# Transposed tiles written back by halves, with four buffers, a later share and smaller loads, in a convolution-attention kernel

## The chip, the cores and the metric

The kernel runs on one core of one Trainium2 chip, as one program with one launch. The metric is the device time of a whole execution in microseconds (us). The kernel before took 1756.65, 1762.4 and 1763.76 us in three runs, so 1762.4 us at the median.

## The reference, cut to what matters

There are four images (B = 4) of 32 channels and 128 x 128 pixels. Layer 0 gathers each 2 x 2 patch of pixels, so that an image has 4096 positions of 128 values, and lets every position attend to all others by the cosine between them. Layer 1 takes the same data as 4096 tokens of 128 values: linear attention over 8 heads, then a mixture of 8 experts of which each token takes 2.

```python
xs = x.reshape(B, C, h, R, w, R).transpose(0, 1, 3, 5, 2, 4).reshape(B, C * R * R, h, w)
q = xs.reshape(B, C * R * R, hw)
...
energy = jnp.einsum('bci,bcj->bij', q, q)
d = jnp.sqrt(jnp.diagonal(energy, axis1=1, axis2=2))
energy = energy / (d[:, :, None] * d[:, None, :])
attn = jax.nn.softmax(energy, axis=-1)
out = jnp.einsum('bcj,bij->bci', q, attn)
out = gamma * out + xs
...
K = jnp.einsum('bnd,hkd->bhnk', x, Wk)
Q = jnp.einsum('bnd,hkd->bhnk', x, Wq)
V = jnp.einsum('bnd,hed->bhne', x, Wv)
KtV = jnp.einsum('bhnk,bhne->bhke', K, V)
out = jnp.einsum('bhnk,bhke->bne', Q, KtV)
...
top_p, top_i = jax.lax.top_k(router_probs, K)
top_p = top_p / jnp.sum(top_p, axis=-1, keepdims=True)
expert_out = jnp.einsum('bnd,edc->bnec', x, expert_w) + expert_b
gathered = jnp.take_along_axis(expert_out, top_i[..., None], axis=2)
return jnp.einsum('bnk,bnkc->bnc', top_p, gathered)
...
t = t + _L1_attn_ref(_ln_t(t), L1_attn_Wk, L1_attn_Wq, L1_attn_Wv)
t = t + _L1_ffn_ref(_ln_t(t), L1_ffn_router_w, L1_ffn_router_b, L1_ffn_expert_w, L1_ffn_expert_b)
```

`energy` is a 4096 x 4096 matrix for each image, and symmetric. Its softmax needs no maximum, since the entries are cosines, so the kernel computes exponentials, sums them by rows and divides at the end. Tokens are normalised ahead of both parts of layer 1, and each part is added to them.

## The kernel before

**Tiling.** The 4096 positions of an image are cut into NCH = 8 chunks of CH = 512, and each chunk into NJ = 4 blocks of 128. Since the matrix of exponentials is symmetric, only the lower half of the chunk pairs is computed: for row i the columns jc = 0 to i (`attend`, L417). One step is one block of 128 x 512: a product on TensorE into `pe` (L556), the exponential on ScalarE into `pr` with its row sum (L559), and the product with the values on TensorE into `po` (L440). Each of these products is float32 and is two matmul records in the profile.

**The transposed half.** A chunk pair off the diagonal also counts for the row jc with its transpose. The transpose is made in two stages. VectorE transposes `pr` by blocks of 32 x 32 into `F` (L369, reached through L566), four instructions for a tile of four steps. The blocks are then put in their places by a way through DRAM: SP issues one DMA that writes the tile (1 MB) to the DRAM tensor `blocks` (`move`, L483), and after it has landed four DMAs that read it back to `G` (`bring`, L491), each to 32 partitions. TensorE then multiplies `G` with the values into `pg`, one block at a time (`transposed_share`, L375); ScalarE sums its rows (L380), and VectorE adds the finished share to the row's output `o` (L385). The diagonal pair goes the same way in a smaller form (`below`, `diagonal_share`).

**Order.** The order of the work on TensorE, VectorE, ScalarE and SP is written out by hand, and each of these engines works through its own in that order. `tick` counts steps; `after(n, f)` issues f that many steps later: the values after 2, the DVE transpose after 1, the write of a tile 2 after its last exponential and the read 3 after that. `clock` counts units of TensorE work, 8 for a step and 4 for a block of a share. A share is put into the list `late` and is due `LAG` = 57 units after its read is issued; one block of it is run at each step (`step_share`, L411), in the order of the list. In the last row of the last image the tiles jc = 3 and 4 do without DRAM: 16 DMAs each move the blocks from F to G directly (L476, `last`), and their shares are due 58 units later. The last two tiles of that row are computed twice instead.

**Buffers.** F and G have three buffers of 8 KB per partition each (`fpool`, `gpool`), `pr` six, `blocks` four. `F`'s are also used by the diagonal and by the end of the kernel, `G`'s also by the `tmp` tiles of the end (L1152).

**What runs beside it.** While image b is in `attend`, other work is woven in as generators. `timed` holds them with a begin and an end in per cent of the image's work and a number of pieces: `prep` of the next image (loads xx by `load_tokens`, four DMAs of 128 KB each, and makes the normalised vectors), `input_rows` (loads the tokens T of the image in four parts of four DMAs), and in image 0 `setup_weights` and `setup_sorting`, which copies the input to two DRAM tensors `xs` in eight parts of 624 KB issued from ScalarE's queue. `steady` holds layer 1 of the image before: from 84% of an image `layer1` closes its rows (`close_rows`), computes the attention, routes the tokens, sorts them by expert through DRAM with indirect DMAs issued by GpSimd (L988, L1113), and stores its output through SP (L1095). Image 3's own layer 1 is done after its attention, by `last_parts`, without sorting.

Of the kernel before, what the change touches and what calls it, by code (L numbers as in the profile page):

```python
# [12 lines left out]
F32 = mybir.dt.float32  # L13
# [9 lines left out]
def kernel(  # L23
# [39 lines left out]

    nc = tc.nc
    P = 128
    B, C, H, W = x.shape
# [15 lines left out]
    big1 = ctx.enter_context(tc.tile_pool(name="big1", bufs=1))  # L85
    opool = ctx.enter_context(tc.tile_pool(name="opool", bufs=NCH))
    ppool = ctx.enter_context(tc.tile_pool(name="ppool", bufs=6))
    fpool = ctx.enter_context(tc.tile_pool(name="fpool", bufs=3))
    gpool = ctx.enter_context(tc.tile_pool(name="gpool", bufs=3))
    work = ctx.enter_context(tc.tile_pool(name="work", bufs=2))  # L90
    stat = ctx.enter_context(tc.tile_pool(name="stat", bufs=2))
    dram = ctx.enter_context(tc.tile_pool(name="dram", bufs=2, space=bass.MemoryType.DRAM))
# [43 lines left out]
    def setup_sorting():  # L136
        def iota(dst, pattern, part=0):
            nc.gpsimd.iota(
                dst, pattern=pattern, base=0, channel_multiplier=part, allow_small_or_imprecise_dtypes=True
            )  # L140

        iota(rank_below, [[1, P]], part=-1)
        nc.vector.tensor_scalar(rank_below, rank_below, 0.0, None, ALU.is_gt)
        iota(upto, [[1, E], [-1, E]])
        nc.vector.tensor_scalar(upto, upto, 0.0, None, ALU.is_ge)
        iota(tiles_of[:, 0, :], [[P, HR]])
        iota(tile_no[:, :, 0], [[1, NT]])
# [134 lines left out]
    def prep(b, kc, st):  # L282
# [17 lines left out]

        def load_half(g, pt):
# [51 lines left out]
    tick = [0]  # L353
    queued = []
    late = []
    LAG = 57
    exps = []

    BELOW = {1: 0, 2: 1, 3: 3}
# [10 lines left out]

    def transposed_share(b, st, i, jc, G):

        pg = ps_g.tile([P, CH], F32, tag="pg", name=f"pg_{b}_{i}_{jc}")
        for ib in range(NJ):
            nc.tensor.matmul(  # L375
                pg.rearrange("p (a f) -> p a f", a=4), st["qT"][i][:, ib, :], G[:, :, ib],
                start=(ib == 0), stop=(ib == NJ - 1),
            )
            junk = work.tile([P, 4, P], BF16, tag="junk", name=f"junk_{b}_{i}_{jc}_{ib}", bufs=1)
# [37 lines left out]
    def attend(b, st):  # L417
# [11 lines left out]
        for i in range(NCH):  # L429
# [37 lines left out]
                    at += P * ib  # L467
                done()

            def move(F, i, jc):  # L470
                last = b == B - 1 and i == NCH - 1 and jc >= NCH - 5
                if last:
                    G = gpool.tile([P, 4, NJ, P], F32, tag="G", name=f"G_{b}_{i}_{jc}")
                    for a in range(4):
                        for q in range(4):
                            nc.sync.dma_start(  # L476
                                G[ts(q, S), a].rearrange("p ib f -> p (ib f)"),
                                F[ts(a, S), q].rearrange("p ib j c -> p (ib j c)"),
                            )
# [3 lines left out]
                nc.sync.dma_start(  # L483
                    blocks.rearrange("a p q f -> (a p) q f"), F.rearrange("p q ib j c -> p q (ib j c)")
                )
                after(3, partial(bring, blocks, i, jc))

            def bring(blocks, i, jc):
                G = gpool.tile([P, 4, NJ, P], F32, tag="G", name=f"G_{b}_{i}_{jc}")
                for q in range(4):  # L490
                    nc.sync.dma_start(  # L491
                        G[ts(q, S)].rearrange("p a ib f -> p a (ib f)"), blocks[:, :, q].rearrange("a p f -> p a f")
                    )
# [34 lines left out]
            for jc in order:  # L528
# [13 lines left out]
                    step_share()  # L542
                    yield
                if jc < i and not both:
                    F = fpool.tile([P, 4, NJ, NJ, S], F32, tag="F", name=f"F_{b}_{i}_{jc}")
                    Fb = F.rearrange("p q ib j c -> p ib q j c")
                elif jc == i and not ending:
                    F = fpool.tile([P, 4, 6, S], F32, tag="F", name=f"F_{b}_{i}_{i}")
                own = []
                for j in range(NJ):  # L550
# [12 lines left out]
                        st["exps"] = True  # L563
                    after(2, partial(values, pr[:, c0:], t, c0, CH))
                    if jc < i and not both:
                        after(1, partial(nc.vector.transpose, Fb[:, :, :, j, :], pr))  # L566
                        if j == NJ - 1:
                            after(2, partial(move, F, i, jc))
                    elif jc == i and not ending:
                        if j < NJ - 1:  # L570
                            after(1, partial(turn_blocks, F, pr, j))
                        if j == NJ - 2:
                            after(2, partial(move_diagonal, F, i))
                    elif jc == i and j in (1, 2):

                        after(1 if j == 2 and order[-1] == i else 2, partial(below, own, (2, 1) if j == 1 else (3,)))
# [742 lines left out]
    for b in range(B):  # L1319

        if b == 0:
            for kc, begin, end in ((1, 0, 5), (2, 6, 20), (3, 25, 45)):
                timed.append((prep(0, kc, states[0]), begin, end, 12))
            timed.append((setup_weights(), 46, 58, 9))
            timed.append((setup_sorting(), 58, 98, 9))
        if b + 1 < B:
            nxt = states[b + 1]
            timed.append((prep(b + 1, 0, nxt), 65, 82, 13))
            timed.append((prep(b + 1, 1, nxt), 83, 99, 13))
        timed.append((input_rows(b, states[b]), *((55, 75) if b in (0, B - 1) else (82, 99)), 9))  # L1330
        done = [0] * len(timed)
        start = clock[0]
        closing = None
# [67 lines left out]
```

## Time and profile before

| | |
|---|---|
| median of three runs | 1762.4 us |
| the profiled execution's own time | 1753.19 us |
| its span, first to last instruction | 1751.4 us |
| granted TensorE clock, mean | 0.983 |
| DMA: bytes moved, mean rate | 355.24 MB, 203 GB/s |
| queue of SP (q1): packets, share of the 16 DMA engines | 219792, 64.0% |
| writes of tiles to DRAM (L483) | 108 of 1024 KB |
| reads of tiles from DRAM (L491) | 432 of 256 KB |
| direct moves (L476) | 32 of 64 KB |
| loads of T and of xx on SP (L279) | 64 and 62 of 128 KB |

The profile is of one execution. A row of its groups names the line, the engine, the operation and the tile written and those read, then the count, the busy time and the mean of one, and then the idle time of the engine just ahead of these instructions with what ended it. TensorE's busy time is modelled from pipelined matmuls: how many of them lie in a stretch says more than the busy share. DMA issues of SP are listed with their tiles; a DMA that SP issues late because it waits delays all that stand behind it in SP's order. The packets of the DMA engines are recorded with queue, size and duration.

### The profile page before, as it was taken

The numbers are of one execution on the slowest core, as the hardware profiler recorded it, in microseconds if no ns is written. First come the engines' busy times: TensorE is split into PE (matmuls) and PEld (weight loads), VectorE is DVE, ScalarE is ACT, GpSimd is POOL, SyncE is SP. The second block draws the span as 40 slices with busy tenths as digits, with TensorE's granted clock in tenths as the row PEclk, the third lists the DMA queues.
The fourth block names the chain that finished last, engine by engine and source line by source line (L and its number), as shares of the span: only waits on it lengthen the run. The fifth ranks groups of instructions, "written<-read, shape, count | busy, mean of one in ns | idle before, by whom it ended". The sixth has DMA issues, their size and how long they took to land. (4 is left out here: it accounts for less than half of the span.)

```text
span 1751.4 us, 21197 instructions
## 1 busy us (share of the span) xinstructions
PE 1667.8 (95%) x5458; PEld 882.2 (50%) x5458; DVE 939.7 (54%) x2443; ACT 927.0 (53%) x2893; POOL 512.0 (29%) x553
## 2 busy tenths in 40 slices
PE   8999998999999999899999999979999999899887
PEld 5444444455554455445554455535555455444633
DVE  4433333467485335566477334546748533455687
ACT  3555444466565555446565455536556455445376
POOL 1000000011026505540015622552102660463166
PEclk9999999999999999999999999989999999999989
DMA  4675877776568799997567799998656889995001
GB/s 136 195 207 166 217 200 222 237 212 190 165 195 239 232 276 252 264 243 197 164 189 223 227 273 264 251 244 224 192 166 196 251 223 271 265 267 133 1 13 37
DMA packets 240168, 355.24 MB, mean 203 GB/s; under 512 B 26928, under 2 KB 154928, under 8 KB 226096
## 3 DMA queue, kind: packets, MB, share of 16 engines
q1 hardware_dynamic: 219792, 314.91, 64.0%
q0 software_dynamic: 12288, 25.19, 5.1%
q10 hardware_dynamic: 7968, 13.77, 2.7%
q8 instruction: 46, 0.75, 0.2%
q14 instruction: 74, 0.61, 0.1%
HBM read 183.64 MB, written 173.15 MB: 204 GB/s over the span
## 5 line engine op out<-in xcount | busy, mean ns | idle before, releaser
L559 ACT ACTIVATE pr<-pe 128x512 f32<-128x512 f32 (+1 forms) x576 | 322.3, 560 | 546.3 <-PE pe L556 427.9
L440 PE MATMUL po<-pr,qT 128*128 128x512 f32 (+3 forms) x1152 | 553.2, 562 | 3.9 <-ACT o L445 3.5
L375 PE MATMUL pg<-G,qT 128*128 128x512 f32 x880 | 456.8, 601 | 37.5 <-DMA G<-blocks 25.6
L556 PE MATMUL pe<-qn,qn 128*128 128x512 f32 x896 | 464.7, 601 | 1.9 <-ACT pr L559 1.6
L369 DVE STREAM_TRANSPOSE F<-pr 128x512 f32<-128x512 f32 x440 | 305.9, 702 | 169.6 <-ACT pr L559 152.2
L440 PEld LDWEIGHTS po<-pr,qT 128*128 128x128 f32 x1152 | 217.1, 192 | 252.6 <-issue 224.8
L380 ACT ACTIVATE junk<-G 128x512 bf16<-128x512 f32 x440 | 273.1, 621 | 33.9 <-DMA G<-blocks 27.3
L375 PEld LDWEIGHTS pg<-G,qT 128*128 128x128 f32 x880 | 167.3, 192 | 239.6 <-issue 205.8
L1113 POOL DMA_INDIRECT yb<-ys,place x192 | 185.1, 964 | 275.6 <-DMA xn<-xs 103.2
L988 POOL DMA_INDIRECT xs<-xn,place x192 | 185.6, 967 | 125.5 <-issue 51.6
L556 PEld LDWEIGHTS pe<-qn,qn 128*128 128x128 f32 x896 | 156.0, 193 | 113.9 <-issue 103.5
L385 DVE TENSOR_TENSOR o<-o,pg 128x512 f32<-128x512 f32 x110 | 75.4, 685 | 201.4 <-PE pg L375 170.1
L164 POOL TENSOR_TENSOR rn<-ss,neg_half 128x8 f32<-128x8 f32 (+1 forms) x17 | 27.8, 1634 | 401.6 <-DVE ss L325 401.6
L559 ACT ACTIVATION_READ_ACCUMULATOR pr<-pe 128x1 f32 x576 | 112.1, 195 | 0.0
L1022 ACT ACTIVATE xn<-pys 128x256 f32<-128x256 f32 (+1 forms) x120 | 44.9, 376 | 116.1 <-PE pys L1055 69.3
L1048 PEld LDWEIGHTS pys<-ew_sb,xn 128*128 128x128 f32 x468 | 67.9, 191 | 57.2 <-issue 45.3
L164 POOL TENSOR_TENSOR rsf<-dm_f,neg_half 128x8 f32<-128x8 f32 (+1 forms) x15 | 26.2, 1746 | 235.1 <-DVE sv_f L635 235.1
L556 PE MATMUL pe<-qn 128*128 128x512 f32 (+3 forms) x256 | 90.2, 435 | 0.7 <-ACT qn L344 0.7
L380 ACT ACTIVATION_READ_ACCUMULATOR junk<-G 128x1 f32 x440 | 84.4, 192 | 0.0
L1048 PE MATMUL pys<-ew_sb,xn 128*128 x468 | 71.8, 276 | 11.4 <-ACT xn L1022 5.4
L1031 DVE COPY result<-pys 128x256 f32<-128x256 f32 (+1 forms) x60 | 24.6, 410 | 101.6 <-ACT xn L1022 46.2
L164 POOL TENSOR_TENSOR rsa<-dm_a,neg_half 128x8 f32<-128x8 f32 x16 | 26.4, 1647 | 167.4 <-DVE sv_a L635 167.1
(189 smaller groups left out, 1618.5 us busy)
## 6 DMA issues: line engine op xcount, KB each, us to landing
blocks<-F SPq DMA_DIRECT2D x108, 1024.0 KB
G<-blocks SPq DMA_DIRECT2D x432, 256.0 KB
xn<-xs SPq DMA_DIRECT2D x114, 128.0 KB
below<-F SPq DMA_DIRECT2D x31, 384.0 KB
G<-below SPq DMA_DIRECT2D x124, 96.0 KB
T<-in_x_dram SPq DMA_DIRECT2D x64, 128.0 KB
out_dram<-acc SPq DMA_DIRECT2D x128, 64.0 KB
xx<-in_x_dram SPq DMA_DIRECT2D x62, 128.0 KB
```

The costliest lines, as they stand in the source:

```text
L164: pinned(nc.gpsimd.tensor_tensor(dst, src, neg_half.to_broadcast(list(src.shape)), ALU.pow))
L369: f()
L375: nc.tensor.matmul(pg.rearrange("p (a f) -> p a f", a=4), st["qT"][i][:, ib, :], G[:, :, ib], start=(ib == 0), stop=(ib == NJ - 1),)
L380: nc.scalar.activation(junk, G[:, :, ib], AF.Copy, accum_out=st["sums"][:, NJ * i + ib, jc : jc + 1])
L385: nc.vector.tensor_tensor(o, o, pg.rearrange("p (a j c) -> p a j c", a=4, c=S), ALU.add)
L440: nc.tensor.matmul(row["po"][:, lo:hi], qT[blk // NJ][:, blk % NJ, :], w, start=start, stop=(row["left"] == 0))
L556: nc.tensor.matmul(pe[:, c0:], qn[jc][:, ts(j, P)], qn[i][:, c0:], start=True, stop=True)
L559: nc.scalar.activation(pr[:, c0:], pe[:, c0:], AF.Exp, accum_out=sums[:, t, i : i + 1]).ins
L988: inst = nc.gpsimd.indirect_dma_start(xs[h], offset(place[:, i, k : k + 1]), xn[:, k, :], None)
L1022: nc.scalar.activation(bufs[4 + g % 2][:, :n], p[:, : n * P].rearrange("p (j t) -> p j t", t=P), AF.Copy)
L1048: nc.tensor.matmul(p[:, 2 * P + j * D : 2 * P + j * D + D], bufs[4 + g % 2][:, j, :], weights[:, bass.ds(begins[2 * (g % 2) + j], D)], sta ...
L1113: inst = nc.gpsimd.indirect_dma_start(yb[k // 4][:, i, k % 4, :], None, ys, offset(place[:, i, k : k + 1]))
```

## The change

A tile of F becomes two half tiles, each of two transposed steps, with four buffers of 4 KB per partition. Each half is written to DRAM by its own DMA as soon as its second transpose is done (`write_half`), to every other kilobyte of `blocks`; the read (`bring`) stays at the tick where it was, five after the last exponential, and waits for both. G keeps its size, has four buffers, and its elements stand in another order within a partition, so that L375 and L380 read runs of 64 elements where they read runs of 128. The share is due 76 units after the read (`LAG`), in the last row of the last image 57 (`LAST_LAG`). The direct moves are gone: those two tiles go through DRAM as well. T and xx are loaded in halves of 64 KB per DMA (the first load of all excepted), the copies to xs in 16 parts, and the loads of T in images 0 and 3 are spread over other stretches. `pr` has six buffers, before and after.

```diff
-    fpool = ctx.enter_context(tc.tile_pool(name="fpool", bufs=3))
-    gpool = ctx.enter_context(tc.tile_pool(name="gpool", bufs=3))
+    fpool = ctx.enter_context(tc.tile_pool(name="fpool", bufs=4))
+    gpool = ctx.enter_context(tc.tile_pool(name="gpool", bufs=4))
...
-        step = NT * P // 4
-        for g in range(8):
-            inst = nc.scalar.dma_start(xs[g // 4][ts(g % 4, step), :], rows[ts(g, step), :])
-            xs_made[g // 4].append(inst.ins)
+        step = NT * P // 8
+        for g in range(16):
+            inst = nc.scalar.dma_start(xs[g // 8][ts(g % 8, step), :], rows[ts(g, step), :])
+            xs_made[g // 8].append(inst.ins)
...
-        load_tokens(
-            xx.rearrange("p k w r -> p k (w r)"), b, 8 * kc, 8, (nc.sync, nc.scalar if first else nc.sync)
-        )
+        rows = xx.rearrange("p k w r -> p k (w r)")
+        if first:
+            load_tokens(rows, b, 0, 8, (nc.sync, nc.scalar))
+        else:
+            load_tokens(rows[:, :4], b, 8 * kc, 4)
...
         yield
         yield
+        if not first:
+            load_tokens(rows[:, 4:], b, 8 * kc + 4, 4)
...
-    LAG = 57
+    LAG = 76
+    LAST_LAG = 57
...
-                pg.rearrange("p (a f) -> p a f", a=4), st["qT"][i][:, ib, :], G[:, :, ib],
+                pg.rearrange("p (a g f) -> p a g f", a=4, g=2), st["qT"][i][:, ib, :], G[:, :, :, ib],
...
-                junk, G[:, :, ib], AF.Copy, accum_out=st["sums"][:, NJ * i + ib, jc : jc + 1]
+                junk, G[:, :, :, ib], AF.Copy, accum_out=st["sums"][:, NJ * i + ib, jc : jc + 1]
...
-            def move(F, i, jc):
-                last = b == B - 1 and i == NCH - 1 and jc >= NCH - 5
-                if last:
-                    G = gpool.tile([P, 4, NJ, P], F32, tag="G", name=f"G_{b}_{i}_{jc}")
-                    for a in range(4):
-                        for q in range(4):
-                            nc.sync.dma_start(
-                                G[ts(q, S), a].rearrange("p ib f -> p (ib f)"),
-                                F[ts(a, S), q].rearrange("p ib j c -> p (ib j c)"),
-                            )
-                    late.append((clock[0] + 58, transposed_share(b, st, i, jc, G)))
-                    return
-                blocks = dram.tile([4, S, 4, CH], F32, tag="blocks", name=f"blocks_{b}_{i}_{jc}", bufs=4)
+            def write_half(blocks, F, g):
                 nc.sync.dma_start(
-                    blocks.rearrange("a p q f -> (a p) q f"), F.rearrange("p q ib j c -> p q (ib j c)")
+                    blocks[:, :, :, g].rearrange("a p q f -> (a p) q f"), F.rearrange("p q ib j c -> p q (ib j c)")
                 )
-                after(3, partial(bring, blocks, i, jc))
 
             def bring(blocks, i, jc):
-                G = gpool.tile([P, 4, NJ, P], F32, tag="G", name=f"G_{b}_{i}_{jc}")
+                G = gpool.tile([P, 4, 2, NJ, 2 * S], F32, tag="G", name=f"G_{b}_{i}_{jc}")
...
-                late.append((clock[0] + LAG, transposed_share(b, st, i, jc, G)))
+                late.append((clock[0] + (LAST_LAG if ending else LAG), transposed_share(b, st, i, jc, G)))
...
-                    F = fpool.tile([P, 4, NJ, NJ, S], F32, tag="F", name=f"F_{b}_{i}_{jc}")
-                    Fb = F.rearrange("p q ib j c -> p ib q j c")
+                    blocks = dram.tile([4, S, 4, 2, CH // 2], F32, tag="blocks", name=f"blocks_{b}_{i}_{jc}", bufs=4)
...
-                        after(1, partial(nc.vector.transpose, Fb[:, :, :, j, :], pr))
-                        if j == NJ - 1:
-                            after(2, partial(move, F, i, jc))
+                        if j % 2 == 0:
+                            F = fpool.tile([P, 4, NJ, 2, S], F32, tag="F", name=f"F_{b}_{i}_{jc}_{j // 2}")
+                        after(1, partial(nc.vector.transpose, F.rearrange("p q ib j c -> p ib q j c")[:, :, :, j % 2, :], pr))
+                        if j % 2:
+                            after(2, partial(write_half, blocks, F, j // 2))
+                            if j == NJ - 1:
+                                after(5, partial(bring, blocks, i, jc))
...
-        for kc in range(4):
-            load_tokens(T[:, ts(kc, 8), :], b, 8 * kc, 8)
+        for k in range(0, KT, 4):
+            load_tokens(T[:, k : k + 4, :], b, k, 4)
...
-            timed.append((setup_sorting(), 58, 98, 9))
+            timed.append((setup_sorting(), 58, 98, 17))
...
-        timed.append((input_rows(b, states[b]), *((55, 75) if b in (0, B - 1) else (82, 99)), 9))
+        timed.append((input_rows(b, states[b]), *((52, 94), (82, 99), (82, 99), (52, 80))[b], 17))
```

More of the change, by code (lines that the diff above doesn't have):

```diff
@@ L375, in transposed_share @@
             nc.tensor.matmul(
-                pg.rearrange("p (a f) -> p a f", a=4), st["qT"][i][:, ib, :], G[:, :, ib],
+                pg.rearrange("p (a g f) -> p a g f", a=4, g=2), st["qT"][i][:, ib, :], G[:, :, :, ib],
                 start=(ib == 0), stop=(ib == NJ - 1),
             )
-            junk = work.tile([P, 4, P], BF16, tag="junk", name=f"junk_{b}_{i}_{jc}_{ib}", bufs=1)
+            junk = work.tile([P, 4, 2, 2 * S], BF16, tag="junk", name=f"junk_{b}_{i}_{jc}_{ib}", bufs=1)
             nc.scalar.activation(
-                junk, G[:, :, ib], AF.Copy, accum_out=st["sums"][:, NJ * i + ib, jc : jc + 1]
+                junk, G[:, :, :, ib], AF.Copy, accum_out=st["sums"][:, NJ * i + ib, jc : jc + 1]
             )
@@ L468, in below @@
                 done()
-            def move(F, i, jc):
-                last = b == B - 1 and i == NCH - 1 and jc >= NCH - 5
-                if last:
-                    G = gpool.tile([P, 4, NJ, P], F32, tag="G", name=f"G_{b}_{i}_{jc}")
-                    for a in range(4):
-                        for q in range(4):
-                            nc.sync.dma_start(
-                                G[ts(q, S), a].rearrange("p ib f -> p (ib f)"),
-                                F[ts(a, S), q].rearrange("p ib j c -> p (ib j c)"),
-                            )
-                    late.append((clock[0] + 58, transposed_share(b, st, i, jc, G)))
-                    return
-                blocks = dram.tile([4, S, 4, CH], F32, tag="blocks", name=f"blocks_{b}_{i}_{jc}", bufs=4)
+            def write_half(blocks, F, g):
                 nc.sync.dma_start(
-                    blocks.rearrange("a p q f -> (a p) q f"), F.rearrange("p q ib j c -> p q (ib j c)")
+                    blocks[:, :, :, g].rearrange("a p q f -> (a p) q f"), F.rearrange("p q ib j c -> p q (ib j c)")
                 )
-                after(3, partial(bring, blocks, i, jc))
             def bring(blocks, i, jc):
-                G = gpool.tile([P, 4, NJ, P], F32, tag="G", name=f"G_{b}_{i}_{jc}")
+                G = gpool.tile([P, 4, 2, NJ, 2 * S], F32, tag="G", name=f"G_{b}_{i}_{jc}")
                 for q in range(4):
                     nc.sync.dma_start(
-                        G[ts(q, S)].rearrange("p a ib f -> p a (ib f)"), blocks[:, :, q].rearrange("a p f -> p a f")
+                        G[ts(q, S)].rearrange("p a g ib f -> p a (g ib f)"),
+                        blocks[:, :, q].rearrange("a p g f -> p a (g f)"),
                     )
-                late.append((clock[0] + LAG, transposed_share(b, st, i, jc, G)))
+                late.append((clock[0] + (LAST_LAG if ending else LAG), transposed_share(b, st, i, jc, G)))
             def move_diagonal(F, i):
```

## The prediction

> **What bounds the kernel now.** I read the busy shares first, then the groups of TensorE's instructions with the idle time ahead of each, then busy time by 25 us windows, and last TensorE and SP in order of time around one of the worst windows.
>
> ```profile
> PE 1667.8 (95%) x5458; PEld 882.2 (50%) x5458; DVE 939.7 (54%) x2443; ACT 927.0 (53%) x2893; POOL 512.0 (29%) x553
> L440 PE MATMUL po<-pr,qT 128*128 128x512 f32 (+3 forms) x1152 | 553.2, 562 | 3.9 <-ACT o L445 3.5 <-issue 0.4
> L375 PE MATMUL pg<-G,qT 128*128 128x512 f32 x880 | 456.8, 601 | 37.5 <-DMA G<-blocks 25.6 <-issue 7.0 <-DVE rdx L699 2.4
> ```
>
> TensorE is the bound with 95%, and nearly half of the 84 us that it idles stands before one matmul, the share of a transposed tile (L375), which waits for G to come back from DRAM. Ahead of the other two matmuls of a step (L440, L556) it idles 6.5 us in all.
>
> ```profile
> 325.00:350.00 25.00, 25.00 (x69) 11.81 (x68) 10.51 (x19) 11.68 (x36) 0.00 (x0) 1.00 0.83 244
> 250.00:275.00 25.00, 17.57 (x41) 7.65 (x41) 5.46 (x8) 8.01 (x24) 0.00 (x0) 0.92 0.91 249
> 725.00:750.00 25.00, 22.45 (x51) 10.19 (x51) 10.33 (x21) 9.17 (x29) 14.62 (x16) 0.87 0.98 249
> 1150.00:1175.00 25.00, 17.27 (x41) 7.59 (x40) 13.67 (x31) 8.01 (x24) 14.10 (x14) 0.87 1.01 249
> ```
>
> First PE busy and matmul count, last the granted clock, the share of the DMA engines and GB/s. Undisturbed, 69 matmul records fit in 25 us; in the late rows of images 0, 1 and 2 it is 41 to 51, and just there the clock falls to 0.87 to 0.92 and the DMA engines are 91% to fully busy.
>
> ```profile
> 1164.54 1.02 PE L556 MATMUL pe<-qn,qn 128*128 128x512 f32 x2
> 1165.39 1.02 PE L440 MATMUL po<-pr,qT 128*128 128x512 f32 x2
> 1172.70 2.04 PE L375 MATMUL pg<-G,qT 128*128 128x512 f32 x2 [6.29 <-DMA G<-blocks]
> 1174.54 1.91 PE L556 MATMUL pe<-qn,qn 128*128 128x512 f32 x2
> 1176.25 1.91 PE L440 MATMUL po<-pr,qT 128*128 128x512 f32 x2
> ```
>
> ```profile
> 1156.27 0.34 SPq L483 DMA_DIRECT2D blocks<-F  x1
> 1156.73 3.31 SPq L1095 DMA_DIRECT2D out_dram<-acc  x4
> 1162.32 2.09 SPq L491 DMA_DIRECT2D G<-blocks  x4
> 1164.51 0.38 SPq L483 DMA_DIRECT2D blocks<-F  x1
> ```
>
> A 512-column matmul (two records) starts 0.85 to 0.86 us after the last one; after a stall of 6.29 us the next ones start 1.7 to 1.84 us apart for some 5 us. A stall is thus paid twice. SP issues in order: the tile's write at 1156.3, its read 6 us later, when the write has landed, and the next tile's write behind that read.
>
> In TensorE's order of time 14 gaps over 0.8 us stand before L375 up to 1585 us: 9.5 us in image 0 (the longest 6.0), 10.4 in image 1, 13.0 in image 2, 4.2 in image 3; sum 37.1. The clock at half speed behind them costs, from the clock records of the trace (half of 3.4 to 10.2 us each, less what lies in a gap), 4.4, 4.9, 4.7 and 1.7: sum 15.7. So 13.9, 15.3, 17.7 and 5.9: **52.8 us** is the ceiling for a change of this round trip.
>
> [...] each read at L491 fills 32 partitions, and the four of a tile take 5.5 to 6.2 us of packet time when alone, 170 to 190 GB/s. [...] here the read's first packet comes about 1.5 us after the write's last. [...] before has no packet of 1 KiB.
>
> **The change part by part.** A step of full blocks is three matmuls, 3 x 0.86 = 2.58 us, a tile four steps, 10.3 us; a unit of the schedule's clock (12 a step) is 0.215 us.
>
> *Round trip before.* The DMA packet records, grouped by size, give for each tile: write alone 3.5 us from issue to last packet (128 packets of 8 KB, 309 ns each at the median, over 16 engines 2.5 us), 1.5 us of nothing, read 6 us: 11 us, and the next write stands behind the read. In rows 6 and 7 that is longer than the 10.3 us of a tile, so the slack between landing and share falls from 12 us to about 1, and any other burst becomes a stall.
>
> *Halves.* At L483 one DMA becomes two, each as soon as two of the four DVE transposes are done; DRAM runs become 1 KB, so 1,024 packets a tile for 128. Price of one: not below the line through the medians of 512 B (27 ns) and 2 KB (84), 46 ns; 512 B writes to DRAM in the tail take 34, so 34 + 512/27 B per ns = 53; not above half of a loaded 2 KB read (145), 72. I take 53: 3.4 us for 2.5, +0.9 us per tile of DMA time. In return the read waits for half as much (1.3 us earlier), and as the first half of the next tile is issued two ticks after this tile's second half, ahead of the read, it fills the 1.5 us of nothing. Net in a DMA-bound stretch +0.6 us per tile. DVE does the same 440 transposes of 703 ns. SP issues 108 more writes of 0.36 us; it waits 271 us for these landings, which hides that.
>
> *Lag 57 to 76.* 19 x 0.215 = 4.1 us more between read and share. G is then held 76 + 48 = 124 units, 10.3 steps; three buffers recycle after 12 steps, four after 16. Alone the lag covers every gap but the two of 6 us. Shares of an image's end come 4.1 us later, and layer 1 with them; it is spread over the next image, and nothing of it is late. The last row keeps 57.
>
> *Four half tiles of F.* A buffer comes back after 8 steps for 12. The first half's transposes run on ticks 1 and 2 of a tile, its write goes at 3, the next use is at 9: 6 ticks, 15 us, for a landing that took 11.0 at worst. DVE would hide a miss of some us (54% busy). Nothing.
>
> *Direct moves.* 32 issues (11.9 + 10.2 us of SP) go, for two tiles through DRAM. Their share was due at 2 ticks + 58 units, now 5 ticks + 57, but it queues behind the tile before, whose share ends later than that: same place. Read lands about 8 ticks after the last exponential for a share at 10. Nothing.
>
> *Loads.* T and xx in halves double 62 + 64 issues to about 250, 512 B packets as before; image 0's T starts at 52% for 55% and ends at 94% for 75%; the copies to xs go in 16 parts of 312 KB. They take away bursts such as 250 to 265 us, where T's and xx's eight loads held SP 13.5 us and the ready read behind them came at 264.7: that is the 6.0 us gap. Cost 124 x 0.45 us of SP, beside its waiting. Four G buffers also serve the tail's tmp tiles, where ACT waits at most 1.6 us for POOL: nothing.
>
> *Sum.* Image 0 has no layer-1 traffic beside it: all but 1 of 13.9, 13 us. Images 1 and 2 are short of DMA time, so credit counts: 4.1 + 1.3 + 0.6 per tile over 9 tiles = 10.8 of 15.3, and over 8 tiles 10.2 of 17.7. Image 3: 5 of 5.9. Together **39 us**. The profiled execution took 1753.2 (span 1751.4), which gives 1714; it lies 9.2 below the median of the runs, so against 1762.4 the forecast is **1723**.
>
> **Rivals.**
> *A: the DMA engines bind in images 1 and 2.* For it: shares of 0.98 and 1.01 there, and the bytes stay. Faster TensorE asks for the same in less time, so only the lag counts: 13 + 4.1 + 4.1 + 3 = 24 us, 1738. Against: idle DMA stretches such as 1146 to 1148 and 1162 to 1164 just before reads.
> *B: slower, through 1 KB packets.* If a strided 1 KB write takes over 67 ns, write and read together (1,024 x 67/16 + 6.0 us) pass the 10.3 us of a tile, and every tile of rows 6 and 7 stalls. At 90 ns: 5.8 + 6.0 = 11.8, 1.5 us for each of 13 tiles in 4 images, 78, less 4 x 4.1 of lag: +62 on a kernel that keeps its other stalls, 1824. Against: 512 B packets at 27 to 35 ns.
> *C: time saved is waited for elsewhere.* POOL's gathers for image 2 end near 1600 us, 17 us before the last share, with POOL 60% busy; if that stream sets the end, or F's buffers hold DVE, nothing is gained: 1760. Against: the chain of waits has POOL at 0%.
>
> **How the numbers follow.** Forecast 0.52 (1700 to 1732), A 0.22 (1732 to 1753), C 0.12 (1753 to 1771), B 0.14 (up to 1824). About 0.5%, 9 us, is what can be told from no change. Faster: 0.52 + 0.22 = 0.74; same 0.12; slower 0.14. Range 1700 to 1764: left out are B, and some of C and of a gain near the ceiling.
>
> **What would show it.** Idle before L375 falls from 37.5 to under 10 us; 250:275 has some 66 matmuls for 41; clock mean above 0.988; packets of 1 KB near 53 ns; SP's wait at the read well under 270.8 us; L385 and the tail from 1620 on unchanged in length. Wrong would be: 1 KB packets over 67 ns (B), L375 still idle in images 1 and 2 with DMA shares over 1.0 (A), or new idle time of DVE for blocks<-F (C).

## The result, and the profile after

The changed kernel took 1782.84 us at the median (1780.09 to 1784.32), the kernel before beside it 1760.97: a ratio of 1.0124, 95% interval 1.0102 to 1.0147. It is slower by 1.2%, 60 us above the forecast and 19 above the range. The profiled execution took 1780.09 us, with a span of 1778.3 and a mean clock of 0.978 (before: 0.983).

The groups of TensorE after (line, tile and inputs, count, then busy time and mean, then the idle time just ahead and what ended it). L547 is the energy matmul (L556 before), L379 the share (L375), L316 the transposes of xx (L313), L1050 the transposes of the sorted tokens (L1055):

```profile
L547 PE MATMUL pe<-qn,qn 128*128 128x512 f32 x896 | 467.6, 604 | 17.7 <-ACT pr L550 17.7
L379 PE MATMUL pg<-G,qT 128*128 128x512 f32 x880 | 457.8, 602 | 22.6 <-DMA G<-blocks 16.0 <-DVE acc L1077 4.3 <-issue 1.0
...
L1050 PE MATMUL pys<-ident,xn 128*128 128x128 f32 x234 | 45.3, 276 | 6.4 <-DMA xn<-xs 6.3
...
L316 PE MATMUL ptq<-ident,xx 128*128 128x128 f32 x128 | 21.9, 299 | 21.8 <-issue 15.6 <-DMA xx<-in_x_dram 6.1
```

The three others of these groups before:

```profile
L556 PE MATMUL pe<-qn,qn 128*128 128x512 f32 x896 | 464.7, 601 | 1.9 <-ACT pr L559 1.6
...
L1055 PE MATMUL pys<-ident,xn 128*128 128x128 f32 x234 | 44.8, 273 | 0.0
...
L313 PE MATMUL ptq<-ident,xx 128*128 128x128 f32 x128 | 21.3, 293 | 5.7 <-DMA xx<-in_x_dram 5.7
```

The wait that the change aimed at did fall, from 37.5 to 22.6 us. But three rows that were nearly empty before (1.9, 0.0 and 5.7 us) now hold 17.7, 6.4 and 21.8. Three of the four windows shown of before, in the same columns (TensorE busy and matmul count first, clock, DMA share and GB/s last):

```profile
250.00:275.00 25.00, 24.48 (x64) 11.17 (x63) 8.87 (x13) 11.86 (x37) 0.00 (x0) 1.00 0.83 236
...
725.00:750.00 25.00, 16.93 (x42) 8.18 (x41) 9.77 (x21) 7.25 (x24) 14.90 (x17) 0.80 0.87 211
1150.00:1175.00 25.00, 17.42 (x44) 8.44 (x43) 9.94 (x22) 7.46 (x25) 15.72 (x17) 0.86 0.90 223
```

Image 0 gained what was forecast for that place: 64 matmul records for 41. As a whole, though, it is only 3.0 us shorter, where the sum has 13: by the starts of the energy matmuls row 6 became 7.8 us shorter, and rows 5 and 7 together 7.4 longer. In the late rows of images 1 and 2 nothing was gained (42 for 51, 44 for 41), and the clock is lower (0.80 for 0.87, 0.86 for 0.87). SP's waits, and one of VectorE's (engine and line, what for, us in total, times, the longest):

```profile
SPq L475 <- DVE F L373: 176.3, 62, 9.6
SPq L482 <- DMA blocks<-F: 142.9, 42, 7.1
...
SPq L475 <- DMA ew_sb<-in_L_ffn_expert_w_dram: 15.8, 1, 15.8
```

```profile
DVE F L373 <- DMA blocks<-F: 28.8, 7, 7.9
```

The first two of them before:

```profile
SPq L491 <- DMA blocks<-F: 270.8, 58, 9.4
...
SPq L483 <- DVE F L369: 91.5, 29, 6.5
```

SP waits half as long for landed writes ahead of its reads, and almost twice as long for VectorE ahead of the writes; VectorE now waits for half tiles of F, as rival C had it. Below, the largest new gap in order of time:

```profile
726.07 1.02 PE L547 MATMUL pe<-qn,qn 128*128 128x512 f32 x2
726.18 3.66 SPq L278 DMA_DIRECT2D xx<-in_x_dram  x4
726.93 1.02 PE L444 MATMUL po<-pr,qT 128*128 128x512 f32 x2
...
735.78 0.52 SPq L475 DMA_DIRECT2D blocks<-F  x1
736.03 1.10 PE L316 MATMUL ptq<-ident,xx 128*128 128x128 f32 x4 [8.07 <-issue]
736.35 1.95 SPq L278 DMA_DIRECT2D xx<-in_x_dram  x3
736.92 1.91 PE L547 MATMUL pe<-qn,qn 128*128 128x512 f32 x2
```

TensorE stands for 8.07 us ahead of the transposes of xx, which SP had begun to load just before, and the next two energy matmul records take 1.91 us where those at 726.07 took 1.02; the granted clock is 0.50 from 731.5 to 741.7 us. No share is near.

### The profile page after: what moved, and what is told of

The parts are those of the page before. It is cut to its first block, busy times and chain, and to the rows that moved or that the text cites. A ratio compares the mean times of both kernels' runs of the same rounds, so it can differ in the third digit from the quotient of the medians.

```text
span 1778.3 us, 21552 instructions
## 1 busy us (share of the span) xinstructions
PE 1673.4 (94%) x5458; PEld 885.7 (50%) x5458; DVE 937.8 (53%) x2443; ACT 921.9 (52%) x2893; POOL 511.6 (29%) x553
## 5 line engine op out<-in xcount | busy, mean ns | idle before, releaser
L547 PE MATMUL pe<-qn,qn 128*128 128x512 f32 x896 | 467.6, 604 | 17.7 <-ACT pr L550 17.7
L379 PE MATMUL pg<-G,qT 128*128 128x512 f32 x880 | 457.8, 602 | 22.6 <-DMA G<-blocks 16.0
L379 PEld LDWEIGHTS pg<-G,qT 128*128 128x128 f32 x880 | 168.0, 194 | 215.3 <-issue 193.9
L547 PEld LDWEIGHTS pe<-qn,qn 128*128 128x128 f32 x896 | 157.0, 193 | 140.2 <-issue 99.3
L547 PE MATMUL pe<-qn 128*128 128x512 f32 (+3 forms) x256 | 90.6, 436 | 0.7 <-ACT qn L347 0.7
L1043 PE MATMUL pys<-ew_sb,xn 128*128 x468 | 72.7, 279 | 11.5 <-ACT xn L1017 7.4
```

The costliest lines, as they stand in the source:

```text
L379: nc.tensor.matmul(pg.rearrange("p (a g f) -> p a g f", a=4, g=2), st["qT"][i][:, ib, :], G[:, :, :, ib], start=(ib == 0), stop=(ib == NJ ...
L547: nc.tensor.matmul(pe[:, c0:], qn[jc][:, ts(j, P)], qn[i][:, c0:], start=True, stop=True)
L1043: nc.tensor.matmul(p[:, 2 * P + j * D : 2 * P + j * D + D], bufs[4 + g % 2][:, j, :], weights[:, bass.ds(begins[2 * (g % 2) + j], D)], sta ...
```

## The experiments

Each is compared with the kernel before, run on the same chip, and different groups of experiments ran on different chips. The figure after the time is its ratio to the kernel before, with the 95% interval; it can differ by 0.1% from the quotient of the two medians. Times of different groups are best compared by these ratios. They are numbered in order, since the expectations refer to each other so.

### 1 to 4: the parts of the change

**1: the changed kernel without its loads.** T, xx and xs again in the parts and windows of before.

> The changed kernel with the loads of T, xx and xs in as few parts, and in the windows, of the kernel before; halves, lag and buffers stay. Theory L (the loads: twice as many transfers on SP's and ScalarE's queues hold up the reads, the prefetch of xx and, through ScalarE's queue, the exponentials): the waits of TensorE at the transposes of xx (21.8 us after, 5.7 before) fall back to about 6, and the time falls by 25 us or more below the changed kernel, to under 1758. Theory H (the halves: more writes on SP, ahead of the reads, and buffers of F that hold VectorE): at most 8 us are saved, 1775 or more. Theory D (the later share) the same as H: 1775 or more.

Measured: 1774.03 us, 1.0052 (1.0034 to 1.0069). The loads cost 0.7% here (1.0052 against 1.0124), 9 to 13 us and not 25, and what is left is still slower than before.

**2: the kernel before with these loads alone.**

> The kernel before with the loads in more parts and their new windows, nothing else. Theory L: slower than before by 15 us or more (1776 or more). Theories H and D: the stall of 6 us in image 0 at 272 us goes and nothing is lost, so 1750 to 1764.

Measured: 1762.59 us, 0.9989 (0.9970 to 1.0007). By themselves they cost nothing that can be measured: theory L falls. The starts of the energy matmuls in the trace show why it is even: row 6 of image 0 became 10.5 us shorter, later rows together longer.

**3: the later share alone.**

```diff
-    LAG = 57
+    LAG = 76
+    LAST_LAG = 57
```

> The kernel before with the share of a transposed tile 76 units after its read for 57 (57 in the last row), three buffers of G as before; whole tiles, direct moves and loads as before. Theories L and H: TensorE's idle time ahead of the share falls from 37.5 to about 15 us and the time to 1725 to 1745. Theory D (shares that come later push other work together and are paid elsewhere): 1760 or more, with new waits ahead of the energy matmul.

Measured: 1766.30 us, 1.0021 (1.0006 to 1.0036): theory D. Its groups of TensorE (one line number higher than before):

```profile
L557 PE MATMUL pe<-qn,qn 128*128 128x512 f32 x896 | 465.9, 602 | 20.7 <-ACT pr L560 20.4 <-issue 0.2
L376 PE MATMUL pg<-G,qT 128*128 128x512 f32 x880 | 453.5, 597 | 11.5 <-DMA G<-blocks 10.7 <-issue 0.7
...
L313 PE MATMUL ptq<-ident,xx 128*128 128x128 f32 x128 | 22.1, 301 | 30.3 <-issue 21.3 <-DMA xx<-in_x_dram 9.0
```

The share's wait fell by 26.0 us, most of what the prediction had, and the kernel is no faster: 18.8 us more stand ahead of the energy matmul, 24.6 ahead of the transposes of xx.

**4: halves alone.** Half tiles, four half buffers, no direct moves; share at 57 units, three buffers of G, loads of before.

> The kernel before with halves of the transposed tiles, four half buffers and no direct moves, the share at 57 units, three buffers of G, loads as before. Theory H: slower by 10 us or more (1772 or more), with waits of VectorE for a buffer of F and of the exponentials for buffers that VectorE holds. Theories L and D: within 10 us of before, 1750 to 1770.

Measured: 1765.45 us, 1.0006 (0.9990 to 1.0022). No cost, and no gain: the wait ahead of the share is 38.8 us in it.

So no part that was tried alone costs more than 0.21%, and together they cost 1.2%. (The fourth buffer of G was not tried alone.) The later share is the part to understand, since its saving is plain in the trace and missing in the time.

### 5 to 8: full DMA engines

**5: the kernel before with T of images 1 and 2 earlier.**

```diff
-        timed.append((input_rows(b, states[b]), *((55, 75) if b in (0, B - 1) else (82, 99)), 9))
+        timed.append((input_rows(b, states[b]), *((55, 75) if b in (0, B - 1) else (44, 64)), 9))
```

> The kernel before with one edit: T of images 1 and 2 is loaded at 44 to 64% of the image for 82 to 99%. Theory S (in the last quarter of images 1 and 2 the DMA engines are full, and the stretch takes as long as their packets do, whoever waits): T's 4,096 packets of 512 bytes leave it, and the time falls by 10 us or more, under 1754. Theory P (the stretch is set by the path of one tile, write, landing, read): no more than 5 us are gained, 1758 or more.

Measured: 1744.27 us, 0.9898 (0.9874 to 0.9921): as theory S forecast, and faster than both kernels. Two windows of image 2, first of the kernel before, then of this one:

```profile
1155.00:1170.00 15.00, 10.54 (x24) 4.48 (x24) 10.02 (x24) 5.30 (x16) 7.97 (x8) 0.95 0.98 230
1170.00:1185.00 15.00, 12.30 (x26) 5.52 (x27) 6.01 (x12) 4.61 (x14) 7.37 (x8) 0.71 1.00 274
```

```profile
1155.00:1170.00 15.00, 15.00 (x42) 7.01 (x41) 11.53 (x25) 7.37 (x24) 9.17 (x9) 1.00 0.94 247
1170.00:1185.00 15.00, 13.58 (x47) 6.98 (x46) 11.52 (x34) 9.12 (x26) 8.66 (x9) 1.00 0.96 296
```

The kernel before had its DMA engines at 0.98 and 1.00 and ran 50 matmul records in these 30 us; with T gone it runs 89 (it is some 10 us ahead by then, so these are not the same steps to the last). Row 7 became 8.4 us shorter in image 1 and 10.2 in image 2.

With T, however, two things leave the stretch: its packets, and its place in SP's order. In the kernel before, SP was held by these loads just ahead of stores and reads of a tile:

```profile
1164.93 5.60 SPq L279 DMA_DIRECT2D T<-in_x_dram  x4
...
1179.15 10.37 SPq L279 DMA_DIRECT2D T<-in_x_dram  x4
1189.61 1.98 SPq L1095 DMA_DIRECT2D out_dram<-acc  x4
1191.70 1.83 SPq L491 DMA_DIRECT2D G<-blocks  x4
```

No run here tells full DMA engines from an SP that is held up.

**6: the later share and T early.**

> The share at 76 units alone, as in the third run, and T of images 1 and 2 at 44 to 64%. Theory S: with the engines relieved the gain of the later share stays: TensorE's wait of 30 us at the transposes of xx falls to under 12, and the time is under 1742, faster than the kernel before by 1% or more. Theory P: 1758 or more.

Measured: 1764.65 us, 1.0005 (0.9989 to 1.0020). A miss for theory S: the later share gives back the whole gain of 5. T's place matters in the kernel before, but it isn't what the later share costs.

**7: the changed kernel with T early.**

> The changed kernel with T of images 1 and 2 at 44 to 64% for 82 to 99%, all else as changed. Theory S: 15 us or more faster than the changed kernel, under 1768. Theory P: within 6 us of it.

Measured: 1773.51 us, 1.0057 (1.0034 to 1.0080): 9 us better than the change, not 15; between the two theories.

**8: the later share, with the transposes of xx later after their load.** `idle(2 if b else 1)` in `prep` becomes `idle(6 if b else 1)`, with four counts more in its windows.

> The share at 76 units alone, and the transposes of xx (which waited 30 us for its load in the third run) four counts of its schedule later after the load, some 11 us. Theory S: the wait goes from these transposes to another consumer of DMA data (the share, or xn from xs), and the time stays within 8 us of the third run's 1766. Theory O (the stall is only a question of the order in which TensorE meets the load): the wait at the transposes falls under 10 us and the time by 20 us or more, under 1746.

Measured: 1773.31 us, 1.0059 (1.0040 to 1.0077). The wait moved, as theory S has it, and the time rose by 7 us:

```profile
L376 PE MATMUL pg<-G,qT 128*128 128x512 f32 x880 | 456.0, 600 | 26.5 <-DMA G<-blocks 22.8 <-issue 2.8 <-DVE F L370 0.9
...
L313 PE MATMUL ptq<-ident,xx 128*128 128x128 f32 x128 | 21.7, 298 | 5.8 <-DMA xx<-in_x_dram 5.8
```

The transposes fell from 30.3 to 5.8 us, the share rose from 11.5 to 26.5.

### 9 to 12: the rate of layer 1

The main loop moves layer 1 on at most once a step, when the clock has gone `PACE` units:

```python
    PACE = 10
...
                for stream in steady:
                    if clock[0] >= stream[1]:
                        stream[1] = clock[0] + PACE
                        moved.append(stream[0])
```

A step of full blocks counts 12 units when it holds a block of a share, 8 when not; after a step of 12 layer 1 moves, after one of 8 it waits for the next. So where the shares fall decides how often layer 1 moves. Counted in the schedule, it is called 833 times before and 872 with the share at 76 units. These counts take in calls of streams that are already through: the work of layer 1 is the same in both, and what differs is at which steps, and how densely, it is done. In image 1, layer 1 of image 0 is called at 122 of the 144 steps before, and at 128 with the later share. Where tokens are scattered or gathered, two indirect transfers go with a call.

**9: the later share with `PACE = 12`.**

> The share at 76 units alone, as in the third run, with layer 1 moved on every 12 units of the schedule's clock for 10. The schedule moves layer 1 at most once a step, when the clock has gone PACE units; counted over the whole program that is 833 moves before, 872 with the share at 76 units (it changes which steps hold a share, and so where the clock passes the mark), and 826 in this kernel. Theory R (the rate: the later share packs layer 1 of the image before, with its two indirect transfers a move and its loads and stores, 5% more densely into the steps, and the denser stretch gives back what the share saves): 15 us or more faster than the third run's 1766, under 1751, and the exponentials' waits beyond their energy matmul fall from 100 us to under 60. Theory S (full DMA engines, whoever asks first): within 8 us of 1766.

Measured: 1763.78 us, 1.0031 (1.0015 to 1.0047). A miss for theory R, although layer 1 is called less often than before (826). The larger mark hardly thinned out the dense stretch: from first to last, the 64 indirect scatters of an image span 36 steps for 35 in experiment 3, and 37 before.

**10: the kernel before with `PACE = 8`.**

> The kernel before with layer 1 moved on every 8 units for 10: 930 moves for 833, 12% denser, all else as before. Theory R: slower than before by 20 us or more, 1783 or more. If the rate of layer 1 doesn't matter: 1755 to 1770.

Measured: 1805.39 us, 1.0250 (1.0220 to 1.0281): the rate of layer 1 can matter, here by more than any other edit.

**11: the later share, T early, `PACE = 12`.**

> The share at 76 units, T of images 1 and 2 at 44 to 64%, layer 1 on every 12 units. Theory R: both gains add, 1742 or less, and at least 18 us under the sixth run's 1765, which has the same share and T with the mark at 10. Theory S: within 8 us of 1765.

Measured: 1768.49 us, 1.0051 (1.0031 to 1.0070). A miss for theory R again.

**12: the changed kernel with `PACE = 12`.**

> The changed kernel with layer 1 on every 12 units: 826 moves for its 872. Theory R: 15 us or more faster than the changed kernel, under 1768, and so about level with the kernel before. Theory S: 1775 or more.

Measured: 1794.32 us, 1.0185 (1.0154 to 1.0217). A miss, and slower than the change itself. So in 9, 11 and 12 fewer calls than before gained nothing: their number alone isn't the cause. A mark is also a coarse tool: it shifts every move after the first.

### 13 to 17: the moves by a table

The moves of one kernel were written down step by step and put into another as a table, so that the place of the shares and the places of the other streams can be changed one at a time.

```diff
-                    if clock[0] >= stream[1]:
+                    if chr(65 + steady.index(stream)) in now_moves:
```

**13: the later share with all moves of before.**

> The share at 76 units alone, and every move of the other streams (layer 1, the prefetches of the next image, T, the set-up) put by a table at the step of the image at which the kernel before has it: only the place of the shares differs from before. Theory M (the later share costs by what it does to the places of the other streams): 15 us or more faster than the third run's 1766, 1750 or less, and faster than before. Theory Q (a share that comes later costs by itself, because TensorE then meets the other engines' lateness at another instruction): 1757 or more.

Measured: 1755.27 us, 0.9960 (0.9918 to 1.0003): 0.6% better than experiment 3, which has the same shares, but between the two theories. Of its five runs three lie from 1752.30 to 1755.27 and two at 1768.39 and 1770.62, and the profiled one is the longest; so the 0.4% below the kernel before is not settled.

**14: the kernel before with the moves of experiment 3.**

> The other half: the share at 57 units as before, and every move of the other streams at the step at which the kernel with the share at 76 units has it (872 moves of layer 1 for 833). Theory M: 1775 or more, slower than before by 1% or more. Theory Q: 1755 to 1769.

Measured: 1792.66 us, 1.0157 (1.0126 to 1.0187): theory M. Nothing is changed but where, and how often, the other streams are moved on, and it costs 28 us (1.57% of 1763). Its groups of TensorE:

```profile
L556 PE MATMUL pe<-qn,qn 128*128 128x512 f32 x896 | 471.7, 609 | 35.5 <-ACT pr L559 35.5
L375 PE MATMUL pg<-G,qT 128*128 128x512 f32 x880 | 458.2, 603 | 13.0 <-DMA G<-blocks 8.2 <-issue 4.8
```

This deserves a second look: the share is due at 57 units as before, and its wait still fell from 37.5 to 13.0 us, in a kernel that is 1.6% slower. The row that the prediction was built on measures who is waited for, not what the waiting costs.

Experiments 3 and 14 also differ in the share alone, with the same places of all else: there the later share gains 1.3% (1.0157 to 1.0021). With the moves of before held it gains 0.4% (13), and with those of experiment 5 it loses 0.3% (0.9898 to 0.9930, experiment 16). What it is worth depends on where the rest stands.

One of the gaps of experiment 14 in order of time, with the energy matmul at 736.27 and the exponential that takes it at 746.66:

```profile
736.27 1.02 PE L556 MATMUL pe<-qn,qn 128*128 128x512 f32 x2
...
742.81 0.96 POOL L1113 DMA_INDIRECT yb<-ys,place  x1 [0.30 <-issue]
...
746.66 0.60 ACT L559 ACTIVATE pr<-pe 128x512 f32<-128x512 f32 x1 [11.62 <-remote]
...
747.40 1.22 PE L556 MATMUL pe<-qn,qn 128*128 128x512 f32 x1 [9.25 <-ACT pr L559]
747.62 0.96 POOL L1113 DMA_INDIRECT yb<-ys,place  x1 [3.85 <-DVE acc L1082]
```

**15: the changed kernel with layer 1's moves of before.**

> The changed kernel with layer 1's moves at the steps of the kernel before; its loads keep their own windows. Theory M: 15 us or more faster than the changed kernel's 1783, 1768 or less. Theory Q: 1776 or more.

Measured: 1773.76 us, 1.0056 (1.0038 to 1.0074): 9 us better, not 15; more than theory Q allows, less than M.

**16: the later share and T early, with the moves of experiment 5.**

> The share at 76 units with T of images 1 and 2 early, all moves at the steps that the fifth run (T early, share at 57 units, 1744) has. Theory M: 1735 or less, faster than the fifth run. Theory Q: 1757 or more, as the sixth run (1765).

Measured: 1751.23 us, 0.9930 (0.9906 to 0.9954): 0.75% better than experiment 6, not faster than experiment 5, and again between the theories. The later share has no gain of its own once T is out of the way.

**17: the changed kernel with the loads and layer 1's moves of before.**

> The changed kernel with the loads of the kernel before and layer 1's moves at the steps of the kernel before: what is left of the change is halves, buffers, no direct moves, and a share at 76 units without its effect on layer 1. Against the fifteenth run (1774) it takes the loads away, against the first (1774, loads away too, 872 moves) the moves. If the moves cost the same here as in the pairs so far (0.6 to 0.75%) and the loads as between the first run and the changed kernel (0.7%): 1758 to 1765, no slower than before by over 0.2%. If the two aren't independent: 1770 or more.

Measured: 1763.04 us, 1.0000 (0.9985 to 1.0014): within the changed kernel the two costs add up. (Put into the kernel before they don't look the same: -0.1% for the loads in experiment 2, 1.6% for the moves in 14.) In pairs that differ in the moves of layer 1 alone or nearly alone (3 and 13, 6 and 16, the change and 15, 1 and 17) the moves cost 0.61, 0.75, 0.68 and 0.52%.

### 18: a faster version

Experiment 5 with one part of the change: in image 0 T in 8 parts over 52 to 94%, and xs in 16 parts.

> The fifth run's kernel (whole tiles, share at 57 units, T of images 1 and 2 at 44 to 64%; 1744) with one part of the change added: T of image 0 in 8 parts over 52 to 94% and xs in 16 parts. In the fifth run image 0 keeps a stall of 6.3 us at 271 us with 3.4 us of half clock behind it, in which the loads of T and xx stood ahead of a read. If those go as in the second run: 1735 to 1741. If the smaller parts only move it: 1742 to 1748.

Measured: 1736.17 us, 0.9850 (0.9832 to 0.9868), faster than the kernel before by 1.5% and than the change by 2.7% (0.9850 over 1.0124). Row 6 of image 0 is 10.0 us shorter than before, where experiment 5 had 0.5; row 7 gives 5.5 of it back.

### Where the time went

From the traces: the stretch from the first to the last of the 64 scatters of an image, and of its 64 gathers, summed over three images, with the steps (energy matmuls of attention) that start in it, and all the rest up to the last step.

| kernel | scatters, us / steps | gathers, us / steps | rest, us / steps | rest per step |
|---|---|---|---|---|
| before | 288 / 111 | 338 / 107 | 1007 / 366 | 2.75 |
| after | 297 / 105 | 343 / 100 | 1021 / 379 | 2.69 |
| 3: later share | 291 / 105 | 337 / 103 | 1016 / 376 | 2.70 |
| 14: its moves alone | 307 / 108 | 345 / 104 | 1022 / 372 | 2.75 |
| 10: `PACE = 8` | 287 / 96 | 321 / 99 | 1087 / 389 | 2.79 |
| 17: loads and moves of before | 306 / 111 | 347 / 107 | 992 / 366 | 2.71 |
| 5: T early | 298 / 111 | 321 / 106 | 1002 / 367 | 2.73 |
| 18 | 299 / 111 | 325 / 107 | 993 / 366 | 2.71 |

The scatters take 287 to 307 us whether 96 or 111 steps run beside them. This stretch hardly gets shorter when fewer steps lie in it (the gathers did by 17 us in experiment 10), so each step packed out of it has to run elsewhere at its full 2.7 us. For the change: its two stretches take 14 us more with 13 steps fewer; the 13 steps cost 13 x 2.75 = 36 elsewhere; the faster share saves (2.75 - 2.69) x 379 = 22 there. 14 + 36 - 22 = 28, and the last step of the trace comes 27 us later (1660 for 1633; the medians are 22 apart, since the profiled execution of before was a short one). That these three terms give the whole is no proof, since they are one subtraction written in parts. The account was read from the traces afterwards, and no run was made to test it. Experiment 10 goes with it: 23 steps fewer in its stretches, 63 us at 2.75, and its last step comes 61 us later. Experiment 14 does so only in part: its last step comes 40 us later, of which 6 steps packed out make 16, while the two stretches themselves took 26 us more.

## Why the prediction was wrong, step by step

**The steps that failed.** Between the forecast, 39 us faster, and the result, 22 us slower, lie 61 us. The largest part, some 39 us, is the gain itself, which did not come: the sum took the idle time ahead of the share, and the half clock behind it (37.1 and 15.7 us in the trace of before, whose clock records show 0.50 in 14 stretches of 3.41 to 10.24 us), as time that the kernel would get back. The share with its moves held gave 7 us of it (13), and with the halves and buffers nothing (17). The rest are two terms that stood at nothing and measured some 12 and 10 us.

The first of these is in the step on **the lag**: "Shares of an image's end come 4.1 us later, and layer 1 with them; it is spread over the next image, and nothing of it is late." What spreads layer 1 over the image is the clock, and the clock counts shares. The later share put layer 1 at other steps, more densely, and that costs 0.5 to 0.75% in the pairs with the later share and 1.6% with the share at 57, where the step had nothing. That the clock counts shares stands in the main loop, where it could have been read. Which of the moved calls cost the time is not shown: fewer calls (9, 11 and 12) did not bring it back, and the old places did, by these 0.5 to 0.75%. The second, the loads, follows below.

**The gain of the lag** was taken at the size of the waits. They did fall by 26.0 us (experiment 3), but with the moves held still the kernel gained 0.4%, 7 us, with an interval that just takes in nothing. Which instruction waits in those stretches says little of what the wait costs. Rival A, that the DMA engines bind there, fits experiment 5, where taking transfers out earned 19 us, but isn't shown by it, since SP's order was relieved too; and it still let the lag earn its 4.1 us an image.

**Halves.** The price was near: where 53 ns were taken, 112,640 packets of 1 KB took 46 at the median, 49 at the mean and 44 at the shortest, and rival B is refuted. (The 84 ns that the prediction took for a packet of 2 KB are the median of ScalarE's queue alone, 3,072 packets; over the whole trace of before the median is 141.) But "+0.6 us per tile" as a credit was not seen: 38.8 us ahead of the share in experiment 4. From experiment 13 to 17, which adds halves, buffers and the end without direct moves, the ratio goes from 0.9960 to 1.0000, which lies within the interval of 13.

**Four half tiles of F: "Nothing".** VectorE waited 28.8 us for them, up to 7.9 at once. The worst landing was priced, not the wait for VectorE ahead of the write, which is SP's longest now. It isn't what sets the change apart from experiment 17, which is level with before and where VectorE waits 28.2 us for them too; what the wait costs in both was not tried alone. Of **the direct moves** no loss shows: nothing was slower in experiment 4 by what can be measured.

**Loads.** "They take away bursts" was right in image 0 (64 records for 41; row 6 10.5 us shorter in experiment 2). "Cost 124 x 0.45 us of SP, beside its waiting" was wrong within the change: 0.7% from experiment 1 to the change, 0.6 from 17 to 15. Two parts of the change aim at one stall: without the loads the row is already 4.8 us shorter in 17, and 8.1 in 15, so most of their gain is taken and their cost stays. Row 7 of image 0 is 6.9 us longer in 15 than in 17. This is read from the traces; no run tried it.

**Rivals.** C named what happened, time saved that is waited for elsewhere, and one of its two reasons, the buffers of F, shows in the trace; the main one it did not have, and it stopped at 1760. The rival that ended slower, B, had a wrong mechanism; none had this one. Of the signs listed, idle before the share under 10 us (22.6), clock over 0.988 (0.978) and the matmul count at 250 (64 for some 66) the first was a poor one: experiment 6 met it with 8.0 us and gained nothing. The end of the kernel was unchanged, as said.

**Added up**, against before: the later share with its moves held -0.4%, halves and buffers +0.4 (13 to 17), loads +0.6 (17 to 15), moves +0.7 (15 to the change): 1.24%. The parts of such a chain add up by construction, and their sizes depend on the order: from before by way of 14 to 3 the moves cost 1.6% and the later share gains 1.3%. The first two are each within the uncertainty of 13.

**What stays open.** Why the exponentials stand so late. From the traces, the delays of those that start over 0.8 us after both their matmul and ScalarE's work before sum to some 35 us before and 125 after. They are no measure of the cost either: in experiment 17, level with before, they sum to 100. In the gap shown, 11.62 us pass and the profile names no releaser. What held that exponential these traces don't tell.

## What to carry to other kernels

Where other work is paced by a counter, an edit that changes what is counted moves that work; look at what advances the counter before costing a delay at nothing, and hold the places fixed by a table to see the edit alone. Idle time ahead of an instruction tells who waits, not what a shorter wait is worth: here the same later share was worth from +0.3 to -1.3% of the time, by where the rest stood, and taking T's loads out of a crowded stretch of the kernel before earned more (0.9898) than moving the wait (1.0021). Two parts that aimed at the same stall cost more together than apart: the loads were worth -0.1% by themselves and cost 0.6 to 0.7% within the change.

## What the runs showed of the hardware that was not expected

The 64 indirect scatters of an image took 95 to 104 us in every kernel, beside 32 to 37 steps; one of GpSimd's takes 0.96 us, and no two of them start less than 1.24 us apart in the traces of before and after, so 64 of them need some 79 us (an estimate from these figures). SP waited 15.8 us ahead of a tile's write for a load of the experts' weights with which it shares no data: in the trace of after the 1,495 transfers that SP and ScalarE issue bear eight completion semaphores (numbers 100 to 107), and SP's wait ahead of that write, which it issued at 176.56 us, was for number 100, which the load bears that ScalarE issued at 172.04. No run tried what that costs.
